# Two ResNet bottlenecks on one core: the Gram stages' transposes shared between TensorE and VectorE

## The chip, the cores and the metric

The kernel runs on one core of a Trainium2 chip, in float32 throughout. The metric is the device time of one execution in microseconds. The kernel before takes 2050.02 us, the median of 3 runs (2049.8 to 2051.2). In what follows PE is TensorE, PEld its loading of weights, DVE is VectorE, ACT is ScalarE, POOL is GpSimd and SP is SyncE, which here only issues transfers.

## The reference

Two bottleneck blocks in a row on a batch of 64 images of 14x14 pixels and 1024 channels (12,544 pixels in all). Each block is, with the batch's own statistics in every normalization:

```python
out = relu(bn(conv1x1(x,   w1) + b1))      # 1024 -> 256
out = relu(bn(conv3x3(out, w2) + b2))      # 256 -> 256
out = bn(conv1x1(out, w3) + b3)            # 256 -> 1024
x   = relu(x + softplus(residual_scale)[0] * out)

# bn: (x - mean) * rsqrt(var + 1e-5) * gamma + beta, mean and var over batch and pixels
```

The third normalization needs mean and variance of the 1024 outputs of the last convolution. The kernel doesn't compute these outputs for that purpose. With z the 256 inputs of that convolution, the variance of an output with weights w is w' G w less the squared mean, where G is the Gram matrix of z over all pixels (256x256) divided by their number. A constant c = max(be2, 0) is taken off z first, which changes no variance and keeps the numbers small.

## The kernel before

All 12,544 pixels of z lie in SBUF as `y_all`, channels on the partitions (two halves of 128). The Gram matrix needs the pixels on the partitions, since TensorE sums over partitions. So each block has a **Gram stage**: 49 times, two blocks of 128 pixels are transposed (four 128x128 transposes on TensorE into a PSUM bank), VectorE copies the bank to an SBUF tile `zt` and takes off c (a row `crow`, loaded by a transfer), and TensorE multiplies `zt` with itself.

```python
def gram(psum, pool, aff, crow, beside):
    g0, g1 = psum.tile(M + 1, "cp"), psum.tile(P + 1, "ap")
    zts = [... for i in range(NZT)]                      # NZT = 4; the last column of each is 1
    def products(k, zt):
        for c in range(CH):                              # CH = 2 blocks of 128 pixels
            nc.tensor.matmul(g0, zt[:, c, 0:P], zt[:, c, :], ...)       # L867: 257 columns
            nc.tensor.matmul(g1, zt[:, c, P:M], zt[:, c, P:], ...)      # L868: 129 columns
    for k in range(NT):                                  # NT = 49
        while normed < NG and normed * GPX < (k + 3) * CH * P:
            ...  norm(s, y_all[:, s, a:b], aff)          # L487, ScalarE: relu(scale * y + shift), 1568 pixels
        tp = psum.tile(CH * M)
        for c in range(CH):
            for s in range(MS):
                nc.tensor.transpose(tp[...], y_all[:, s, px], ident)    # L885
        zt = zts[k % NZT]
        nc.vector.tensor_tensor(zt[:, :, :M], tp..., crow..., ALU.subtract)   # L887
        if before is not None:
            products(*before)
        if k in beside:
            beside[k]()
        before = k, zt
```

`beside` is other work that is put between the pairs: in the first block's Gram stage GpSimd prepares the transformed 3x3 filters of the second block, four pieces (`filters`, lines 160 to 211: some 36 additions and scalings, six results that are sent to HBM as `u`), and at pair 44 VectorE forms sums of w1 and w3 (`combine`, lines 138 to 141) for the fast products that follow. The first block's own filters are prepared by VectorE, half a piece at a time, beside the first convolution. After the Gram stage `conv3_stats` makes mean and variance from G, then the stage follows that does the last convolution of block 0 and the first of block 1 together (`fused`); in block 1 it is the last convolution alone (`final`). In both, GpSimd adds some of the partial sums (lines 425, 430 and 451):

```python
def after7(self):
    u3 = self.saved(...)                                                   # L278, ScalarE, from PSUM
    nc.gpsimd.tensor_add(self.part(1, 1), self.part(1, 1), u3)             # L425
def after3(self):
    self.add(0, 1, self.p)                                                 # L404, VectorE
    nc.gpsimd.tensor_add(v, v, self.u12)                                   # L430
```

The call in the main loop:

```python
crow = pool.tile([P, M], FP, tag="crow", name="crow")
nc.sync.dma_start(out=crow, in_=pars[b][:, NPAR:])
tc.keep_in_program_order(nc.vector.tensor_scalar(crow, crow, 0.0, None, ALU.max))
def piece(s, o):
    spare = [xpool.tile([P, CS * PX], FP, tag="x", name="spare") for i in range(2)]
    for _ in filters(nc.gpsimd, 1, s, o, spare):
        pass
...
beside = {NT - 5: combined}
if b == 0:
    beside.update({1 + 12 * i: partial(piece, i // MS, i % MS) for i in range(MS * MS)})
grams = gram(psum, pool, aff, crow, beside)
made = [conv3(psum, 0, o, w3) for o in range(2)]
...
conv3_stats(psum, pool, grams, w3, ccol, mv3)
```

Where an instruction isn't in `keep_in_program_order`, a scheduler decides when the kernel is built in which order an engine's instructions stand; each engine then runs its list in that order.

Of the kernel before, what the change touches and what calls it, by code (L numbers as in the profile page):

```python
# [38 lines left out]
P = 128  # L40
# [12 lines left out]
NT = NPX // (CH * P)  # L53
NZT = 4
# [26 lines left out]

NROW = M
# [3 lines left out]
def bottlenecks(ctx: ExitStack, tc: tile.TileContext, x, w1s, w2s, w3s, pars, out):  # L86
# [40 lines left out]
    def load_w1(pool, b):  # L127

        w = pool.tile([P, MS, 2, CS // 2, P], FP, tag="w1", name=f"w1_{b}")
        for h in range(2):  # L130
            for o in range(MS):
                nc.scalar.dma_start(out=w[:, o, h], in_=w1s[b][:, o, h])
        return w

    def combine(pool, name, a):

        s = [pool.tile(a[0][0].shape, FP, tag=f"{name}s{i}", name=f"{name}s{i}") for i in range(4)]
        tc.keep_in_program_order(nc.vector.tensor_add(s[0], a[1][0], a[1][1]))
        nc.vector.tensor_sub(s[1], s[0], a[0][0])
        tc.keep_in_program_order(nc.vector.tensor_sub(s[2], a[0][0], a[1][0]))  # L140
        nc.vector.tensor_sub(s[3], a[0][1], s[1])
        return a, s

    def combine_w1(pool, w):
        return combine(pool, "w1", [[w[:, o, h] for h in range(2)] for o in range(MS)])

    def combine_w3(pool, w):
        n = CS // 2
        return combine(pool, "w3", [[w[:, s, o * n : (o + 1) * n] for s in range(MS)] for o in range(2)])
# [10 lines left out]
    def filters(eng, b, s, o, spare):  # L160
# [7 lines left out]
        nc.sync.dma_start(out=g, in_=w2s[b][:, s, o])  # L168

        def scaled(to, v, by):  # L170
            eng.tensor_scalar(to, v, by, None, ALU.mult)  # L171

        eng.tensor_tensor(even, g[:, 0], g[:, 2], ALU.add)
        scaled(quad, g[:, 2], 4.0)
        eng.tensor_tensor(quad, quad, g[:, 0], ALU.add)
# [9 lines left out]
        for i, (row, more, op, by) in parts.items():  # L185
# [3 lines left out]
            if more is not None:  # L189
                v = rest[:, :w]  # L190
                eng.tensor_tensor(v, row, more, op)
                row = v
            if i in FOUR:
                r0, r1, r2 = (row[:, k * P : (k + 1) * P] for k in range(3))
                ends = rest[:, w : w + P]
                eng.tensor_tensor(ends, r0, r2, ALU.add)
                eng.tensor_tensor(u[:, SUM], ends, r1, ALU.add)
                eng.tensor_tensor(u[:, DIFF], ends, r1, ALU.subtract)
# [3 lines left out]
            else:  # L202
# [3 lines left out]
                eng.tensor_tensor(  # L206
# [3 lines left out]
            if i == 2:  # L210
                yield
# [643 lines left out]
    def gram(psum, pool, aff, crow, beside):  # L855
# [6 lines left out]
        normed = 0  # L862

        def products(k, zt):
            for c in range(CH):
                first, last = k == 0 and c == 0, k == NT - 1 and c == CH - 1
                nc.tensor.matmul(g0, zt[:, c, 0:P], zt[:, c, :], start=first, stop=last)  # L867
                nc.tensor.matmul(g1, zt[:, c, P:M], zt[:, c, P:], start=first, stop=last)  # L868

        before = None  # L870
        for k in range(NT):
            while normed < NG and normed * GPX < (k + 3) * CH * P:

                px = [normed * GPX, (normed + 1) * GPX]
                if normed == 0:
                    px.insert(1, CH * P)
                for a, b in zip(px, px[1:]):
                    for s in range(MS):
                        norm(s, y_all[:, s, a:b], aff)
                normed += 1  # L880
            tp = psum.tile(CH * M)
            for c in range(CH):
                px = slice((k * CH + c) * P, (k * CH + c + 1) * P)
                for s in range(MS):
                    nc.tensor.transpose(tp[:, (c * MS + s) * P : (c * MS + s + 1) * P], y_all[:, s, px], ident)  # L885
            zt = zts[k % NZT]
            nc.vector.tensor_tensor(  # L887
                zt[:, :, :M], tp.rearrange("p (c m) -> p c m", c=CH),
                crow[:, None, :].to_broadcast([P, CH, M]), ALU.subtract,
            )  # L890
            if before is not None:
                products(*before)
            if k in beside:
                beside[k]()
            before = k, zt
        products(*before)
        return g0, g1

    def conv3_stats(psum, one, grams, w3, ccol, mv):
# [8 lines left out]

        m = one.tile([P, MS, 2], FP, tag="zmean", name="zmean")
        for s, d in ((0, g0[:, M:]), (1, g1[:, P:])):  # L910
            nc.vector.tensor_copy(m[:, s, 1:2], d)
            nc.vector.tensor_add(m[:, s, 0:1], d, ccol[:, s : s + 1])
        quad = psum.tile(3 * CS, "ax").rearrange("p (o k) -> p o k", k=3)
# [14 lines left out]
        for o in range(CS):  # L928
            for s in range(MS):
                matmul(quad[:, o, 0:2], w3[:, s, o, :], m[:, s, :], start=(s == 0), stop=(s == MS - 1))  # L930
        for o in range(CS):
            matmul(quad[:, o, 2:3], q[:, 0, o * P : (o + 1) * P], ones, start=True, stop=True)
        r = small.tile([P, CS, 3], FP, tag="quad", name="quad")
        nc.vector.tensor_copy(r, quad)
        nc.vector.tensor_copy(mv[:, :, 0], r[:, :, 0])
        sq = small.tile([P, CS], FP, tag="sq", name="sq")
        nc.vector.tensor_mul(sq, r[:, :, 1], r[:, :, 1])
        nc.vector.tensor_sub(mv[:, :, 1], r[:, :, 2], sq)
# [158 lines left out]
    with tc.tile_pool(name="first", bufs=1) as one, tc.tile_pool(  # L1097
# [3 lines left out]
        w1 = load_w1(one, 0)  # L1101
# [6 lines left out]
        w1 = combine_w1(one, w1)  # L1108

        for t, xt in enumerate(pair):  # L1110
# [4 lines left out]
        quarters = itertools.product(range(MS), range(MS))  # L1115
        work = itertools.chain.from_iterable(
            itertools.chain(filters(nc.vector, 0, s, o, spare), (None,)) for s, o in quarters
        )

        def items():  # L1120
            for t in range(2, T, 2):
                xs = [load_x(xpool, 0, t + i) for i in range(2)]
                yield Conv1(psum, one, xs, (t, t + 1), w1, par[0], stats1)
                next(work, None)
# [4 lines left out]
    for b in range(2):  # L1129
        pb = par[b]  # L1130
        sp = softplus(pb)
        ccol = keep.tile([P, MS], FP, tag="ccol", name="ccol")
        nc.vector.tensor_scalar(ccol, pb[:, BE2 : BE2 + MS], 0.0, None, ALU.max)
# [5 lines left out]
        with tc.tile_pool(name=f"last_{b}", bufs=1) as one, tc.tile_pool(  # L1139
# [3 lines left out]
            if b == 0:  # L1143
                w1 = load_w1(one, b + 1)
            aff = affine(aggregate(stats2, 0), MS, pb, G2, BE2)
            with ExitStack() as scope:
# [4 lines left out]
                with tc.tile_pool(name=f"gram_{b}", bufs=1) as pool:  # L1151
                    crow = pool.tile([P, M], FP, tag="crow", name="crow")
                    nc.sync.dma_start(out=crow, in_=pars[b][:, NPAR:])
                    tc.keep_in_program_order(nc.vector.tensor_scalar(crow, crow, 0.0, None, ALU.max))

                    def piece(s, o):
                        spare = [xpool.tile([P, CS * PX], FP, tag="x", name="spare") for i in range(2)]
                        for _ in filters(nc.gpsimd, 1, s, o, spare):
                            pass
# [3 lines left out]
                    def combined():  # L1163
                        if b == 0:
                            weights.append(combine_w1(one, w1))
                        weights.append(combine_w3(one, w3))

                    beside = {NT - 5: combined}
                    if b == 0:
                        beside.update({1 + 12 * i: partial(piece, i // MS, i % MS) for i in range(MS * MS)})  # L1170
                    grams = gram(psum, pool, aff, crow, beside)
                    made = [conv3(psum, 0, o, w3) for o in range(2)]
                    mv3 = small.tile([P, CS, nc.vector.BN_AGGR_DIM], FP, tag="mv3", name="mv3")
                    conv3_stats(psum, pool, grams, w3, ccol, mv3)
# [52 lines left out]
```

## Time and profile before

The profiled execution spans 2048.9 us from its first to its last instruction. By stages:

| stage | from, us | length, us | what it does |
|---|---|---|---|
| first convolution, block 0 | 0 | 313 | products of w1, filters of block 0 on VectorE |
| 3x3 convolution, block 0 | 313 | 299 | |
| Gram stage, block 0 | 612 | 96 | transposes and products, filters of block 1 on GpSimd |
| statistics, first tiles | 708 | 47 | |
| fused last and first convolution | 755 | 575 | |
| 3x3 convolution, block 1 | 1330 | 299 | |
| Gram stage, block 1 | 1629 | 92 | |
| statistics, last convolution | 1721 | 327 | |

How to read the views: the page gives the busy time of each engine and the chain of work that ended last, followed back from the last instruction. The groups of instructions give, for a line of the kernel, how often it ran, its total busy time and the mean of one in ns. The table of windows gives busy times within stretches of time. The timeline gives instructions in order of time, those of one line merged, with the idle time before them in brackets and what ended it. Matmuls overlap in the records, so their pace is read from the differences of their starts. A float32 matmul is recorded as two instructions.

### The profile page before, as it was taken

What the parts mean: (1) busy time and instruction counts of PE and PEld (TensorE: products, weight loads), DVE (VectorE), ACT (ScalarE), POOL (GpSimd) and SP (SyncE); (2) the same over time, 40 slices, a digit from 0 to 9 for tenths busy, and PEclk for the clock granted to TensorE, in tenths of its full rate; (3) what the DMA queues carried; (4) which work ended last, traced back from release to release, by engine and by line L of the source; (5) the groups of instructions that cost most, each with busy time, mean ns of one, the idle gap of its engine ahead of it and who ended that gap; (6) DMA issues with size and microseconds to landing.
All of it is one profiled execution on the core that took longest, in us unless ns stands there. A gap on an engine that the chain in (4) does not pass through costs nothing.

```text
span 2048.9 us, 27957 instructions
## 1 busy us (share of the span) xinstructions
PE 1988.1 (97%) x9896; PEld 1679.1 (82%) x9896; DVE 1559.7 (76%) x2892; ACT 906.4 (44%) x1847; POOL 664.2 (32%) x736
## 2 busy tenths in 40 slices
PE   8989999999989979999999999999999899999998
PEld 4555557999989769999999999989999898555554
DVE  6875568999983556777677667699999734799997
ACT  1101114466644035555555555444656530555555
POOL 0100001121219964333333333312121100566665
PEclk9999999999999989999999999999999999999999
DMA  7755525565642254444444444255656420599998
GB/s 274 271 188 185 189 95 165 185 192 179 198 144 89 96 189 158 187 160 189 158 189 160 187 162 185 95 186 184 199 176 203 173 88 1 219 325 337 339 337 298
DMA packets 160890, 385.88 MB, mean 188 GB/s; under 512 B 8560, under 2 KB 129648, under 8 KB 144240
## 3 DMA queue, kind: packets, MB, share of 16 engines
q1 hardware_dynamic: 150720, 315.88, 44.5%
q10 hardware_dynamic: 5904, 51.91, 6.1%
q0 software_dynamic: 4128, 16.32, 2.0%
q8 instruction: 78, 1.28, 0.2%
q14 instruction: 60, 0.49, 0.1%
HBM read 268.21 MB, written 115.87 MB: 187 GB/s over the span
## 4 chain that ended last, share of the span: by engine, by line
PE 73%; DVE 12%; POOL 6%; DMA 4%; issue 3%; ACT 1%; SPq 0%; DVEq 0%; POOLq 0%; ACTq 0%
PE ay L158 14%; PE cy L158 13%; PE ap L158 7%; PE cp L158 6%; PE even L158 5%; PE odd L158 5%; PE m L158 5%; PE l L158 4%; PE ax L158 4%; PE cx L158 4%; POOL spare L171 3%; PE cp L867 2%; DVE x L404 2%; DMA x<-mid 2%; PE ps L158 1%
## 5 line engine op out<-in xcount | busy, mean ns | idle before, releaser
L278 ACT ACTIVATE cu<-cy,scale 128x196 f32<-128x196 f32 (+1 forms) x552 | 257.5, 475 | 297.5 <-PE cy L158 289.9
L543 POOL TENSOR_TENSOR diffs<-r 128x448 f32<-128x448 f32 (+1 forms) x80 | 111.3, 1402 | 616.9 <-DVE r L525 266.9
L278 ACT ACTIVATE x<-x,shift 128x392 f32<-128x392 f32 x368 | 211.9, 614 | 74.9 <-POOL x L430 58.7
L404 DVE SCALAR_TENSOR_TENSOR x<-cp,scale,x 128x196 f32<-128x196 f32 (+1 forms) x368 | 178.0, 484 | 83.1 <-PE cp L158 81.7
L158 PE MATMUL cy<-ct,w3s 128*128 128x196 f32 (+1 forms) x736 | 222.1, 383 | 2.5 <-ACT cu L278 2.5
L425 POOL TENSOR_TENSOR x<-x,cu 128x196 f32<-128x196 f32 (+1 forms) x184 | 167.3, 909 | 172.1 <-ACT cu L278 172.0
L158 PE MATMUL ay<-at,w1s 128*128 128x196 f32 (+1 forms) x752 | 209.7, 382 | 0.6 <-ACT au L278 0.6
L430 POOL TENSOR_TENSOR x<-x,cu 128x392 f32<-128x392 f32 x124 | 125.7, 1014 | 189.5 <-DVE x L404 189.4
L158 PEld LDWEIGHTS ay<-at,w1s 128*128 128x128 f32 x752 | 136.7, 191 | 35.0 <-ACT au L278 1.5
L158 PEld LDWEIGHTS cy<-ct,w3s 128*128 128x128 f32 x736 | 134.0, 191 | 36.9 <-ACT cu L278 4.1
L278 ACT ACTIVATE au<-ay 128x196 f32<-128x196 f32 (+1 forms) x141 | 53.9, 382 | 244.6 <-PE ay L158 223.2
L451 POOL TENSOR_TENSOR x<-x,cu 128x392 f32<-128x392 f32 x120 | 125.0, 1042 | 82.6 <-DVE x L404 77.5
L158 PE MATMUL m<-sums,ua 128*128 128x224 f32 (+1 forms) x752 | 145.5, 336 | 0.0
L158 PE MATMUL cy<-y,w 128*128 128x196 f32 (+1 forms) x416 | 131.2, 403 | 1.9 <-DVE x L948 1.9
L158 PEld LDWEIGHTS m<-sums,ua 128*128 128x128 f32 x752 | 131.4, 189 | 0.2
L404 DVE SCALAR_TENSOR_TENSOR x<-cx,scale,x 128x196 f32<-128x196 f32 (+1 forms) x184 | 89.1, 484 | 51.8 <-PE cx L158 51.6
L158 PE MATMUL cx<-y,w 128*128 128x196 f32 (+1 forms) x404 | 126.2, 398 | 0.0
L867 PE MATMUL cp<-zt 128*128 128x257 f32 x392 | 120.7, 390 | 5.4 <-DVE zt L887 5.4
L158 PE MATMUL even<-v,ub 128*128 128x224 f32 (+1 forms) x640 | 123.8, 334 | 0.8 <-ACT even L637 0.8
L158 PE MATMUL odd<-v,ub 128*128 128x224 f32 (+1 forms) x640 | 123.9, 335 | 0.2
L158 PE MATMUL l<-diffs,ub 128*128 128x224 f32 (+1 forms) x640 | 122.0, 333 | 0.0
L158 PE MATMUL cy<-ct,w 128*128 128x196 f32 (+1 forms) x368 | 111.2, 384 | 6.6 <-ACT cu L278 6.6
(230 smaller groups left out, 4430.4 us busy)
## 6 DMA issues: line engine op xcount, KB each, us to landing
x<-in_x SPq DMA_DIRECT2D x62, 1568.0 KB, 6.6
ub<-u SPq DMA_DIRECT2D x80, 768.0 KB, 4.6
x<-mid SPq DMA_DIRECT2D x32, 1568.0 KB, 10.2
mid<-x ACTq DMA_DIRECT2D x31, 1568.0 KB, 5.1
out<-x SPq DMA_DIRECT2D x124, 392.0 KB, 6.5
ua<-u SPq DMA_DIRECT2D x96, 256.0 KB, 2.9
ub<-u SPq DMA_DIRECT2D x16, 1024.0 KB, 6.1
u<-y POOLq DMA_DIRECT2D x20, 256.0 KB, 7.0
```

Of the source, the lines that this page charges most:

```text
L158: tc.keep_in_program_order(nc.tensor.matmul(*args, **kw))
L171: eng.tensor_scalar(to, v, by, None, ALU.mult)
L278: tc.keep_in_program_order(nc.scalar.activation(*args, **kw))
L404: nc.vector.scalar_tensor_tensor(v, bank, self.scale[:, o : o + 1], v, ALU.mult, ALU.add)
L425: nc.gpsimd.tensor_add(self.part(1, 1), self.part(1, 1), u3)
L430: nc.gpsimd.tensor_add(v, v, self.u12)
L451: nc.gpsimd.tensor_add(v, v, self.u12[:, i * self.n : (i + 1) * self.n])
L543: nc.gpsimd.tensor_sub(diffs, r[:, :, :, :WH], r[:, :, :, WH:])
L867: nc.tensor.matmul(g0, zt[:, c, 0:P], zt[:, c, :], start=first, stop=last)
```

## The change

Three quarters of the pixels are no longer transposed on TensorE. VectorE has a transpose of blocks of 32x32, which leaves each block within its 32 partitions. So 16 transfers within SBUF first move the pixels: from each quarter of the partitions (32 channels) and each of four runs of 384 pixels to a quarter of the partitions of a tile (`home`), so that partition quarter i of the tile holds all 256 channels of run i. A **step** is 4 x 384 = 1536 pixels, enough for six VectorE transposes of 128x512 elements, each of which fills one `zt`. There are six steps in each Gram stage, two homes in turn, 12 pairs ahead of them and one after them still go by TensorE. Ten of the 16 transfers are issued by SP, six by GpSimd.

Since no copy from PSUM is left in which c could be taken off, c is taken off z in place (`less`), and z stays so: ScalarE does it for the large groups of block 0, VectorE for the rest. A constant taken off every z moves each output by a constant, which the normalization removes, so `conv3_stats` gets simpler. `crow` and its transfer go.

The GpSimd work on filters goes too, since GpSimd has transfers to issue: two of the four pieces of block 1 are prepared by VectorE in the first stage (six pieces in place of four, in smaller parts), two by VectorE in the first Gram stage. The weight sums move from pair 44 to the end. Program order is kept for the transposes, products and filters of the Gram stage. There are six `zt` in place of four, and w1 of block 1 is loaded by SP instead of ScalarE.

The core of the diff:

```diff
-NT = NPX // (CH * P)
-NZT = 4
+NZT = 6
+FIRST, LAST = 12, 1
+RUN = 3 * P
+STEP = 4 * RUN
+STEPS = (NPX - (FIRST + LAST) * CH * P) // STEP
 ...
-    def gram(psum, pool, aff, crow, beside):
+    def gram(psum, pool, homes, aff, less, beside):
 ...
+        bounds = [0, CH * P, 3 * CH * P, *range(GPX, NPX + 1, GPX)]
+        for a, e in zip(bounds, bounds[1:]):
+            for s in range(MS):
+                y = y_all[:, s, a:e]
+                norm(s, y, aff)
+                less(s, y)
+
+        def spread(k):
+            x = homes[k % 2][:, : MS * STEP].rearrange("p (s j f) -> p s j f", s=MS, j=4)
+            for i, j in itertools.product(range(4), range(4)):
+                queue = nc.gpsimd if (4 * i + j) % 8 in (2, 5, 7) else nc.sync
+                a = start + k * STEP + i * RUN
+                queue.dma_start(out=x[32 * i : 32 * i + 32, :, j], in_=y_all[32 * j : 32 * j + 32, :, a : a + RUN])
+            return x.rearrange("p s j f -> p (s j) f")
+
+        def by_tensor(a):
+            tp = psum.tile(CH * M)
+            ...                                  # four transposes on TensorE, kept in program order
+            zt = next(zts)
+            nc.vector.tensor_copy(zt[:, :, :M], tp.rearrange("p (c m) -> p c m", c=CH))
+            return zt
+
+        def by_vector(x, i):
+            zt = next(zts)
+            tc.keep_in_program_order(
+                nc.vector.transpose(
+                    zt[:, :, :M].rearrange("p b (n c) -> p b n c", c=32),
+                    x[:, :, i * CH * 32 : (i + 1) * CH * 32].rearrange("p n (b r) -> p b n r", r=32),
+                )
+            )
+            return zt
+
+        def pairs():
+            for i in range(FIRST):
+                yield by_tensor(i * CH * P)
+            for k in range(STEPS):
+                x = ready.pop(0)
+                for i in range(RUN // (CH * 32)):
+                    yield by_vector(x, i)
+                if k + 2 < STEPS:
+                    ready.append(spread(k + 2))
+            for i in range(LAST):
+                yield by_tensor(NPX - (LAST - i) * CH * P)
+
+        ready = [spread(k) for k in range(2)]
 ...
-        quarters = itertools.product(range(MS), range(MS))
+        pieces = [(0, 0, 0), (0, 0, 1), (0, 1, 0), (0, 1, 1), (1, 0, 0), (1, 0, 1)]
+        total, free = (1 + NF) * len(pieces), T // 2 - 1 - CS // MS      # 42 parts over 11 items
 ...
+                    def less(k, y):
+                        if b == 0 and y.shape[-1] == GPX:
+                            nc.scalar.activation(y, y, AF.Identity, bias=minus_c[:, k : k + 1])
+                        else:
+                            nc.vector.tensor_scalar(y, y, minus_c[:, k : k + 1], None, ALU.add)
+                    ws = sums_tile(one, 2 - b)
+                    homes = [x_tile("home") if b else ws.rearrange("p i n -> p (i n)"), x_tile("home")]
 ...
-                    beside = {NT - 5: combined}
+                    beside = {FIRST + STEPS * RUN // (CH * 32): combined}
                     if b == 0:
-                        beside.update({1 + 12 * i: partial(piece, i // MS, i % MS) for i in range(MS * MS)})
+                        second = x_tile("spare")
+                        work = [filters(nc.vector, 1, 1, o, (x_tile("spare"), second), pinned=True) for o in range(MS)]
+                        ...
+                        beside.update({1 + 3 * i: partial(next, work) for i in range(MS * NF)})
```

The cuts leave out the forms of `combine`, `filters` and `conv3_stats` that follow from this.

## The prediction

> **What bounds the kernel now.** I began with the page: busy shares, then the chain that ended last.
>
> ```profile
> PE 1988.1 (97%) x9896; PEld 1679.1 (82%) x9896; DVE 1559.7 (76%) x2892; ACT 906.4 (44%) x1847; POOL 664.2 (32%) x736
> ...
> PE 73%; DVE 12%; POOL 6%; DMA 4%; issue 3%; ACT 1%; SPq 0%; DVEq 0%; POOLq 0%; ACTq 0%
> ```
>
> TensorE works for 97% of the span, so time can come only from PE work removed (31 to 32 us are at stake here, below) or from its 61 us of idleness. The 6% of POOL in the chain is a hint: GpSimd computes little, yet it stands in the way somewhere. To find where, I cut the span into stages (table of windows; columns are the stretch, its length, then busy us of PE, PEld, DVE, ACT, POOL, PE clock, DMA share, GB/s):
>
> ```profile
> 29.60:313.00 283.40, 276.98 (x832) 158.65 (x831) 197.32 (x335) 31.19 (x60) 13.27 (x24) 0.99 0.50 183
> ...
> 612.30:708.30 96.00, 90.22 (x589) 83.05 (x590) 41.33 (x60) 26.04 (x18) 86.64 (x136) 0.95 0.23 86
> 708.30:755.00 46.70, 36.38 (x142) 25.78 (x141) 24.94 (x56) 10.65 (x23) 39.02 (x58) 0.85 0.53 188
> 755.00:1330.00 575.00, 574.72 (x3466) 574.31 (x3464) 403.36 (x895) 312.28 (x733) 217.97 (x244) 1.00 0.43 168
> ...
> 1629.30:1721.50 92.20, 90.22 (x589) 83.06 (x590) 36.56 (x56) 26.04 (x18) 0.00 (x0) 0.95 0.23 95
> ```
>
> The two Gram stages (612 to 708 and 1629 to 1721) are bound by PE, with DVE under half busy and DMA a quarter used: there is room to move work off PE. The 47 us behind the first one lose 10 us of PE. The timeline of PE inside a Gram stage gives the price of one pair of 128-pixel blocks (start, duration, then the group; overlapping durations, so I read the starts):
>
> ```profile
> 643.45 0.60 PE L885 MATMUL cy<-ident,y 128*128 128x128 f32 x4
> 643.89 0.60 PE L867 MATMUL cp<-zt 128*128 128x257 f32 x2
> 644.32 0.39 PE L868 MATMUL ap<-zt 128*128 128x129 f32 x2
> 644.55 0.60 PE L867 MATMUL cp<-zt 128*128 128x257 f32 x2
> 644.98 0.38 PE L868 MATMUL ap<-zt 128*128 128x129 f32 x2
> 645.20 0.60 PE L885 MATMUL ay<-ident,y 128*128 128x128 f32 x4
> ```
>
> One pair takes 645.20 - 643.45 = 1.75 us; its four transposes take 643.89 - 643.45 = 0.44 us, its products 1.31 us. 49 pairs are 85.8 us; the first stage runs from 613.0 to 708.3, 95.3 us, so 9.5 us are losses: 1.63 and 1.83 us of waiting for DVE at 700 and 704 (DVE had put the eight weight sums of L138 to L141 in front of the zt that PE needed), the rest the slow clock and the waits at the start. The second stage, 1630.0 to 1721.45, loses 5.6 us.
>
> Behind the first Gram stage the chain and PE's timeline show:
>
> ```profile
> 742.77 1.83 POOL spare L171 x3
> ...
> 746.06 0.61 POOL x L425
> ...
> 749.16 1.02 PE L158 MATMUL cy<-ct,w 128*128 128x196 f32 x2 [6.62 <-ACT cu L278]
> ```
>
> GpSimd works through four pieces of block 1's 3x3 filters until 745 and only then does the first addition of the residual (L425). PE waits 6.62 us for what hangs on that, and then runs at half clock until 754.9 (the same matmul of 196 columns steps 0.65 us there, 0.33 after), 2.9 us more.
>
> [...] The PSUM read of the same 512 elements, which it replaces, took 0.69 us (L887). [...] whole-width transfers here reach 337 to 339 GB/s in the last stage. [...]
>
> **The change part by part.**
>
> *Transposes.* Of 49 pairs, 12 + 1 stay on PE, 36 go to DVE. PE saves 36 x 0.44 = 15.8 us per stage, 31.6 in both, if it stays fed.
>
> *What feeds it.* A step is six pairs: 1536 pixels x 256 channels x 4 B = 1.57 MB in 16 transfers. PE uses a step in 6 x 1.31 = 7.9 us, so the transfers must bring 200 GB/s. [...] Latency is covered: six zt buffers let DVE be a step ahead, so a home is free when PE begins on it and its next content is due two steps (15.8 us) later. [...]
>
> *DVE.* [...] 36 x 0.65 = 23 us. With 13 copies (8), two filter pieces (10 us each: for four in the first stage the rows are L171 17.2, L191 8.8, L196 to L198 17.2, L173, L175 and L206 6.1 us, 49 in all, of which some 0.07 us of each of 144 instructions overlap with the next) and a few us of subtractions: 55 of 75 us in the first Gram stage. In the second, 16 subtractions of 1568 elements at about 0.9 us (0.36 us for 384 in L171, scaled) in place of the filters: 47 of 75. Not the bound.
>
> *ACT.* Norm took 26.04 us for 25,088 columns, 1.63 us for 1568. In the first stage ACT also subtracts c for seven groups: 14 more of 1.63 us, 49 us in all. Group 2, which step 0 needs, is done 17 us after ACT's start; plus 8 us of transfer, 25. PE gets through its 12 own pairs in 12 x 1.75 + 6 of start = 27. Just in time. FIRST = 12 looks chosen for this.
>
> *No crow.* The first zt waited for the DMA of crow (landing at 632.3, 1.0 us after the transposes were done, similar in the other stage); a subtraction of 0.3 us takes its place: -0.7 us each, -1.5.
>
> *Weight sums at the end.* They stand behind the last zt now, beside the 2.6 us of conv3 that PE does anyway: -3.5 us.
>
> *GpSimd freed.* No filters there any more: -6.6 of waiting, -2.9 of slow clock. I count -8, since the first units of that stage also wait for ACT (1.35 us at 736.7) and will find something else.
>
> *Filters on DVE in the first stage.* Six pieces in place of four, spread over 11 items of 18.4 us: 42 parts x 1.67 us / 11 = 6.4 us an item, beside 10.3 us of its own: 16.7 of 18.4. PE lost 4.8 us there to DVE waiting for a filter's outgoing transfer, and some 3 us of clock. There were three such changes of piece, now five. +2.
>
> Sum: -31.6 - 1.5 - 3.5 - 8 + 2 = -42.6; +3 for the DMA edge, as an expectation: about -40, **2010 us**.
>
> **Rivals.** (a) *The DMA becomes the bound of the Gram stages.* [...] At 120 GB/s a step takes 13 us, each stage grows by 6 x 5 = 30 us: 2070. (b) *DVE or its fixed order becomes the bound.* If a 32x32 transpose of f32 took 1.3 us, 36 would be 47 us, and the first stage 79 of 75: a few us slower there, 2020. (c) *The saving is there but the first stage gives it back*: DVE full to 91%, in program order, stalls at each of five changes of piece; 5 x 3 us would make 2020 to 2025. (d) *GpSimd was not what held the start of the fused stage*, and x's load or ACT takes its place: 8 us less gain, 2018. The chain speaks against it, being GpSimd without a gap for 45 us.
>
> **Range and chances.** 2% is 2009.0 us, right at my estimate. If all goes as in the sum without the DMA term, 2007; the terms that can fail (a mild, c, d) are each worth 8 to 15 us and have about one chance in four each, and they only add. 1999 would need more from clock and first stage than I count. So 1999 to 2030; faster by over 2%: 0.44, within: 0.51, slower: 0.05, which is rival (a) in earnest.
>
> **What would show it.** Right: Gram stages of about 75 us each with PE products stepping 1.31 us per pair without waits on zt; L885 at 104 instead of 392 transposes; DVE transposes near 0.65 us; step transfers of under 8 us; no PE wait over 2 us between 720 and 760. Wrong: PE waiting for DVE zt which waits for the DMA into home or ws (rival a); DVE busy without gaps in the Gram stage (b); PE waits on DVE y or at in the first 313 us above 8 us (c); a 5 us hole at the start of the fused stage (d).

## The result, and the profile after

| | before | after |
|---|---|---|
| time, median of 4 runs (lowest to highest) | 2049.91 us (2048.19 to 2051.2) | 2023.49 us (2021.36 to 2026.12) |
| ratio, with its 95% interval | 1 | 0.9872 [0.9855, 0.9889] |
| profiled span | 2048.9 us | 2022.6 us |

The changed kernel is 26.4 us faster, 1.3%. The prediction's range held it; its point, 2010, asked for 40 us, so 13.6 us of the expected gain are missing. The page of the changed kernel, busy times and the chain that ended last:

```profile
PE 1955.8 (97%) x9608; PEld 1647.0 (81%) x9608; DVE 1603.2 (79%) x3070; ACT 927.8 (46%) x1865; POOL 599.5 (30%) x648
...
PE 51%; DVE 8%; DMA 4%; SPq 1%; issue 1%; ACT 1%; POOL 0%; DVEq 0%; ACTq 0%; POOLq 0%
```

TensorE lost 32.3 us of busy time (1988.1 less 1955.8) with the 288 transposes that are gone (9896 less 9608 instructions); the time fell by less. GpSimd is out of the chain. Now the same five stages as in the prediction, by windows (stretch, its length, then busy us of PE, PEld, DVE, ACT, POOL, PE clock, DMA share, GB/s):

```profile
29.60:318.50 288.90, 277.19 (x830) 158.12 (x829) 214.65 (x416) 30.62 (x60) 19.76 (x36) 0.99 0.54 195
617.80:703.80 86.00, 75.82 (x445) 67.86 (x446) 56.68 (x141) 47.05 (x34) 25.96 (x48) 0.95 0.77 237
703.80:740.30 36.50, 33.81 (x142) 23.50 (x141) 22.96 (x56) 10.71 (x23) 4.21 (x5) 0.91 0.20 82
740.30:1315.30 575.00, 574.71 (x3466) 574.32 (x3464) 403.27 (x895) 311.74 (x733) 218.17 (x244) 1.00 0.43 166
1617.90:1694.60 76.70, 73.59 (x445) 66.48 (x446) 49.08 (x72) 26.16 (x20) 23.25 (x36) 0.96 0.68 206
```

The two Gram stages do the same products, yet the first has 86.0 us for 75.8 us of TensorE work, the second 76.7 for 73.6. VectorE is at 66% in the first, and still something there waits. Where nothing waits, a pair steps exactly as predicted. TensorE's timeline (start, duration, group), the first products of two pairs in a row:

```profile
661.58 0.60 PE L167 MATMUL cp<-zt 128*128 128x257 f32 x2
...
662.89 0.60 PE L167 MATMUL cp<-zt 128*128 128x257 f32 x2
```

From 661.58 to 662.89 is 1.31 us, a pair without its transposes. The ledger, read from starts of TensorE's instructions at the stage borders (first 3x3 matmul, first transpose of each Gram stage, first conv3 matmul behind it, first matmul of the fused stage's steady part, end):

| stretch | before | after | difference |
|---|---|---|---|
| start to the first 3x3 matmul | 317.1 | 322.6 | +5.5 |
| 3x3 convolution of block 0 | 295.9 | 295.9 | 0 |
| first Gram stage | 95.3 | 85.3 | -10.0 |
| from there to the fused stage's steady part | 48.8 | 38.6 | -10.2 |
| fused stage and 3x3 convolution of block 1 | 873.0 | 876.3 | +3.3 |
| second Gram stage | 91.45 | 76.0 | -15.5 |
| the rest | 327.5 | 328.0 | +0.5 |
| sum (entries are rounded) | 2048.9 | 2022.6 | -26.3 |

Two entries miss the prediction by much: the first Gram stage (75 expected) and the first stretch (+2 expected). The +3.3 does not come again: the twelve other profiles below, in which that stretch's code is the same, have 872.9 to 876.0, eleven of them under 875.

**The first Gram stage.** The timeline of all engines there, cut to VectorE's lines, with TensorE's answer as the last:

```profile
638.69 0.69 DVE L910 COPY zt<-cy 128x512 f32<-128x512 f32 x1 [1.06 <-PE cy L904]
640.44 0.69 DVE L910 COPY zt<-ay 128x512 f32<-128x512 f32 x1 [1.06 <-PE ay L904]
...
644.97 0.70 DVE L916 STREAM_TRANSPOSE zt<-ws 128x512 f32<-128x512 f32 x1
...
646.67 1.41 DVE L189 TENSOR_TENSOR spare<-spare 128x384 f32<-128x384 f32 x4
...
650.65 1.89 DVE L916 STREAM_TRANSPOSE zt<-ws 128x512 f32<-128x512 f32 x3
...
651.41 1.22 PE L167 MATMUL cp<-zt 128*128 128x257 f32 x2 [3.58 <-DVE zt L916]
```

Through the last six of the twelve pairs that TensorE transposes, VectorE idles 1.06 us in each. Behind them stands a heap of filter parts (L186, L189), from 645.6 to 650.65 between the second and the third 32x32 transpose, and TensorE waits 3.58 us for it. Behind the wait it also has less clock, 0.83 granted from 650 to 660 us where the 10 us before have 1.00, by estimate from these two 1.7 us more. The filter parts and the transposes are held in program order, the copies L910 are not: the scheduler put parts behind copies in front of which they were written.

**The start of the fused stage.** The timeline of all engines: GpSimd's first addition there, and TensorE where it had waited 6.62 us:

```profile
732.95 1.10 POOL L442 TENSOR_TENSOR x<-x,cu 128x196 f32<-128x196 f32 x1 [2.06 <-ACT cu L295]
...
735.64 0.49 PE L167 MATMUL ay<-x,w 128*128 128x196 f32 x2
...
736.55 0.60 PE L167 MATMUL cy<-ct,w 128*128 128x196 f32 x2 [0.42 <-ACT cu L295]
```

GpSimd's addition waits for its data now, not the data for it; the hole is 0.42 us. A second loss is gone that the prediction had not seen. In the kernel before, TensorE also waited here:

```profile
730.79 1.55 PE L158 MATMUL cy<-y,w 128*128 128x392 f32 x4 [1.89 <-DVE x L948]
```

VectorE's chain from the sums of the statistics to the first use of their result took 7.3 us there (722.2 to 729.5), with GpSimd at its filters beside it; in the changed kernel it takes 3.2 us (718.5 to 721.7), and 3.2 in the run all by TensorE below, where GpSimd has no filters either. One scaling of 128x8 elements in it (L1177, now L1231) took 1.02 us before and takes 0.23 and 0.22.

**The first stage.** From the table of waits up to 322 us (engine and group waited for, us in total, times, longest):

```profile
DVE y L189 <- DMA u<-y: 14.1, 3, 6.9
...
PE ap L167 <- DVE y L346: 10.5, 5, 4.9
```

In the kernel before, the same two rows had 6.8 us (once) and 5.2 us (twice).

### The profile page after: what moved, and what is told of

The parts are those of the page before. It is cut to its first block, busy times and chain, and to the rows that moved or that the text cites. A ratio compares the mean times of both kernels' runs of the same rounds, so it can differ in the third digit from the quotient of the medians.

```text
span 2022.6 us, 27698 instructions
## 1 busy us (share of the span) xinstructions
PE 1955.8 (97%) x9608; PEld 1647.0 (81%) x9608; DVE 1603.2 (79%) x3070; ACT 927.8 (46%) x1865; POOL 599.5 (30%) x648
## 4 chain that ended last, share of the span: by engine, by line
PE 51%; DVE 8%; DMA 4%; SPq 1%; issue 1%; ACT 1%; POOL 0%; DVEq 0%; ACTq 0%; POOLq 0%
PE cy L167 13%; PE ay L167 9%; PE cp L167 8%; PE ap L167 5%; PE cx L167 4%; DMA x<-mid 3%; PE even L167 3%; PE odd L167 3%; PE ax L167 3%; PE m L167 2%; PE l L167 2%; DVE x L421 1%; DMA out<-x 1%; SPq L896 1%; DVE x L479 1%
## 5 line engine op out<-in xcount | busy, mean ns | idle before, releaser
L421 DVE SCALAR_TENSOR_TENSOR x<-cp,scale,x 128x196 f32<-128x196 f32 (+1 forms) x368 | 177.9, 483 | 82.4 <-PE cp L167 81.3
L167 PE MATMUL cy<-ct,ws 128*128 128x196 f32 (+1 forms) x736 | 221.8, 383 | 2.5 <-ACT cu L295 2.5
L167 PE MATMUL ay<-at,ws 128*128 128x196 f32 (+1 forms) x752 | 209.3, 381 | 1.0 <-ACT au L295 1.0
L167 PEld LDWEIGHTS ay<-at,ws 128*128 128x128 f32 x752 | 136.6, 190 | 35.4 <-ACT au L295 1.9
L167 PEld LDWEIGHTS cy<-ct,ws 128*128 128x128 f32 x736 | 133.6, 190 | 36.9 <-ACT cu L295 3.8
L167 PE MATMUL ap<-x,ws 128*128 128x196 f32 (+1 forms) x376 | 107.5, 390 | 10.2 <-DVE y L346 10.2
```

Of the source, the lines that this page charges most:

```text
L167: tc.keep_in_program_order(nc.tensor.matmul(*args, **kw))
L421: nc.vector.scalar_tensor_tensor(v, bank, self.scale[:, o : o + 1], v, ALU.mult, ALU.add)
```

## The experiments

All times are medians against the kernel before on the same chip; stage lengths come from the one profile of each run, read at the same borders as in the ledger. A stage begins with its first transpose, so a wait in front of that is not in its length.

| run | time (ratio, 95% interval) | first 3x3 matmul at | first Gram | second Gram |
|---|---|---|---|---|
| after | 2023.49 (0.9872 [0.9855, 0.9889]) | 322.6 | 85.3 | 76.0 |
| copies in order | 2060.58 (1.0046 [1.0031, 1.0061]) | 325.5 | 99.4 | 98.6 |
| no filters in Gram | 2013.83 (one run) | 319.9 | 80.7 | 75.2 |
| all by TensorE | 2038.78 (0.9944 [0.9929, 0.9959]) | 322.3 | 89.7 | 90.6 |
| own scratch | 2028.75 (0.9904 [0.9887, 0.9921]) | 326.8 | 85.5 | 76.1 |
| -c apart | 2024.42 (0.9867 [0.9852, 0.9882]) | 323.1 | 85.2 | 77.3 |
| apart and copies | 2021.8 (0.9853 [0.9838, 0.9867]) | 325.2 | 81.3 | 78.0 |
| four pieces | 2018.34 (0.9836 [0.982, 0.9853]) | 315.75 | 86.2 | 75.9 |
| scratch in turns | 2016.59 (0.9826 [0.9811, 0.9841]) | 315.2 | 85.8 | 77.2 |
| turns, apart, copies | 2012.63 (0.9814 [0.98, 0.9828]) | 313.7 | 81.9 | 77.3 |
| c on GpSimd | 2019.2 (0.9839 [0.9822, 0.9856]) | 316.9 | 90.2 | 76.75 |
| one queue | 2036.57 (one run) | 314.1 | 92.6 | 88.7 |
| even queues | 2018.78 (0.9838 [0.9822, 0.9855]) | 313.7 | 90.1 | 75.6 |

### What the transposes are worth: all by TensorE

```diff
-FIRST, LAST = 12, 1
+FIRST, LAST = 48, 1
```

No steps of transfers are left then, only the rest of the change.

> All 49 pairs are transposed by TensorE, with no step of transfers and no 32x32 transposes; the rest of the change (c subtracted from z, filters away from GpSimd, weight sums at the end) stays. Theory: the 36 transposes of a pair are worth 36 x 0.44 = 15.8 us a stage, so the second Gram stage goes from 76.0 to about 91.8; the first, where 9.9 us were lost to VectorE's heap, goes from 85.3 to about 93, and the time to about 2047, so that all else in the change together is worth only about 3 us (GpSimd freed -10, first stage +5.5, the loss at the second block +3). Rival (the waits and not the transposes made the gain): the second stage stays under 85 and the time under 2035.

The second Gram stage took 90.6 us, so the 36 transposes moved to VectorE are worth 14.6 us there (15.8 expected). The first took 89.7, so there they are worth 4.4 us only: this is where the gain went. I had expected 93 for that stage and 2047 in all; it came to 2038.78. Of the 8 us, 3.3 are this stage's: with a copy for every pair the filter parts fell between the copies by themselves and no wait for zt was left in it. Another 2.7 are the stretch in block 1, where the +3.3 is gone, and 1.2 the second stage (91.8 expected). So the rest of the change, which I had put at 3 us, brings 11.5 (2050.28, the kernel before on that chip, less 2038.78).

### Is it the order on VectorE? Copies in order

```diff
-            nc.vector.tensor_copy(zt[:, :, :M], tp...)
+            tc.keep_in_program_order(nc.vector.tensor_copy(zt[:, :, :M], tp...))
```

> The 13 copies of the pairs that TensorE transposes are held in program order on VectorE too, as the filter parts and the 32x32 transposes are already; nothing else differs. Theory (order on VectorE): in the first Gram stage the filter parts of the first twelve pairs were put behind the copies and then stood in one heap of 5 us in front of the third 32x32 transpose; in program order they fit into the 1.06 us that VectorE idles per pair. So that stage falls from 85.3 to 77 to 79 us, TensorE's waits for zt there from 8.7 us to under 2, and the time from 2023.5 to about 2016; the second Gram stage stays at 76. Rival (transfers): the steps are paced by 16 transfers that take about 10 us from first issue to landing, for 7.9 us of products; then the waits only move to the transposes that wait for the transfers, the stage stays at 84 to 86 and the time at 2023.

It came to 2060.58, slower than the kernel before. Waits in that run, of VectorE in the first Gram stage and of TensorE in the second:

```profile
DVE minus_c L1180 <- ACT y L1201: 18.6, 1, 18.6
...
PE cp L167 <- DVE zt L911: 24.4, 1, 24.4
```

The edit removed the heap and made two new waits. In the first stage an instruction of 0.17 us that belongs to the next block (its -c, written into the one buffer that both blocks share) stood in VectorE's queue in mid-stage and could run only when ScalarE had read the old -c for the last time; everything behind it stood for 18.6 us. In the second stage the ordered copies came behind all 16 subtractions of c, and those wait for ScalarE's norm one after the other. So this run tells nothing for or against the order as the cause; it shows what one misplaced instruction of 0.17 us cost in VectorE's queue: 18.6 us for all that stood behind it. The changed kernel has that stray instruction too, with 4.08 us of idle before it, which raised a second theory:

```profile
664.88 0.17 DVE L1178 TENSOR_SCALAR minus_c<-par 128x2 f32<-128x2 f32 x1 [4.08 <-ACT y L1199]
```

### Is it the stray instruction? -c apart, then with the copies

```diff
-        minus_c = keep.tile([P, MS], FP, tag="minus_c", name="minus_c")
+        minus_c = keep.tile([P, MS], FP, tag=f"minus_c_{b}", name="minus_c")
```

> The -c of the two blocks get a buffer each; in the changed kernel they share one, and the 0.16 us instruction that writes the second block's -c was put into VectorE's queue in the middle of the first Gram stage, where it must wait until ScalarE has read the first block's -c for the last time (VectorE idle 4.1 us before it at 665 us; 18.6 us in the run with the copies in order). Nothing else differs. Theory (a stray instruction in the queue): the first Gram stage falls by 2 to 4 us, from 85.3 to 81 to 83, the time to about 2020.5; VectorE's wait for ScalarE before that instruction is gone. Rival (transfers pace the stage): VectorE then waits 4 us for the transfers into home and ws in its place, and the stage and the time stay within 1 us of 85.3 and 2023.

The stage stayed at 85.2 us, the time within 1 us. The rival's numbers were right. The wait for ScalarE is gone and the stage as long as it was, so those 4 us of idle were not on the path: VectorE's 32x32 transposes now stand 5.1 us for a home's transfer and 5.1 for TensorE to give a zt back. The next run adds the copies in order, in the first Gram stage alone:

> A buffer for each block's -c, as in the run with that alone, and the copies from PSUM in program order in the first Gram stage only (in the second, that order had put all 16 subtractions ahead of the first copy and cost 24.4 us). Theory (order on VectorE): the filter parts go into the 1.06 us gaps between copies, the heap of 5 us in front of the third transpose goes away and so does the stray instruction; the first Gram stage takes 77 to 80 us, the second stays at 76, the time is about 2016. Rival (transfers): 84 to 86 us and 2023; a stage between 80 and 84 would say that both take part.

81.3 us, between the two theories' numbers, where the text had said that both take part. TensorE's waits for zt in that stage, in the changed kernel (first row) and in this run:

```profile
PE cp L167 <- DVE zt L916: 8.7, 6, 3.6
...
PE cp L167 <- DVE zt L918: 3.8, 5, 1.3
PE cp L167 <- DVE zt L910: 2.1, 2, 1.8
```

8.7 us of waiting for 32x32 transposes became 3.8, and 2.1 of waiting for the first copies are new: the heap was worth 4 us in this profile, and the same 4 us appear again between the two later kernels without and with this edit (85.8 and 81.9). By the timed runs alone it isn't settled: the interval 0.9838 to 0.9867 overlaps that of the changed kernel.

### The bound below: no filters in the first Gram stage

```diff
         def scaled(to, v, by):
-            run(eng.tensor_scalar(to, v, by, None, ALU.mult))
+            if not pinned:
+                eng.tensor_scalar(to, v, by, None, ALU.mult)
```

The same for the other helper; the two pieces' loads are replaced by zeros from GpSimd.

> Leaves out work: the arithmetic and the weight loads of the two filter pieces in the first Gram stage; what is stored for them is zeros, so the second block's 3x3 convolution is not the reference's. VectorE has 20 us less in that stage. If VectorE (by its order or by its load) held the products back, the stage takes 76 to 78 us, as the second does. If the transfers did, it stays at 84 to 86. If this run shows 77 and the one with the copies in order shows 77 too, the order was the cause and not the load; if only this one does, it was the load.

80.7 us, but 5.3 of them are my own doing: the transposes of the twelfth pair start 26.65 us after the stage's first, in the changed kernel 21.33. TensorE waited 2.3, 2.0 and 0.5 us there for the first subtractions (0.8 in the changed kernel), and had less clock, 0.50 and 0.75 granted in the stage's first two 8 us against 0.67 and 1.00. The reason for the waits stands in two rows of that run's timeline:

```profile
615.76 6.65 DVE L1203 TENSOR_SCALAR y<-y,minus_c 128x256 f32<-128x256 f32 x3 [0.67 <-ACT y L506]
616.49 2.85 POOL L179 MEMSET spare<- 128x3136 f32 x1
```

Three subtractions of 256 and 512 elements, at most 0.5 us each in other runs, needed 6.65 us beside GpSimd's four memsets, which ran without a gap from 611.2 to 622.1. Less these 5.3 us the stage is at 75.4, close to the predicted length and to the second stage in this run, 75.2. So the stage's loss hangs on the filters. It need not be their 23 us on VectorE alone: this run also issues eleven of their twelve stores at once (622.3 to 628.4 us), ahead of the first step, where the changed kernel has them between the steps.

The order explains 4 us of 10 net. Behind the start it explains more. From the transposes of the twelfth pair to its end the stage took 64.0 us in the changed kernel, 57.7 with the copies in order, 54.1 here, and 54.6 in the changed kernel's second stage. There the order was worth 6.3 us, of which 2.3 were lost again at the start, where the ordered copies came late. About 3 us are left for the filters' load, their stores, and transfers that start late (below); how these divide is not shown.

### The first stage: is VectorE too full, or does it wait?

```diff
+            if odd:
+                g = own.tile([P, 3 * w], FP, tag="g", name="g")
+            u5 = own.tile([P, 4 * P], FP, tag=f"u5_{odd}", name="u5")
...
+        def ahead():
+            made = [filters(nc.vector, *piece, spare, own=one, odd=i % 2) for i, piece in enumerate(pieces)]
+            for i, piece in enumerate(made):
+                for following in made[:2] if i == 0 else made[i + 1 : i + 2]:
+                    next(following)
+                yield from piece
```

This is the second form, scratch in turns; the first, own scratch, had two homes for the loaded weights and one new buffer u5.

> First stage only: the filters' loaded weights get two buffers of their own, each load issued one piece ahead, and the last of the six parts of a piece gets a buffer of its own, so that the next piece need not wait until it is stored; the arithmetic and its amount on VectorE stay. Theory (changes of piece): three waits of VectorE for an outgoing transfer, 14.1 us in all and up to 6.9 each, made TensorE late; without them the first 3x3 matmul comes at 317 to 318 us in place of 322.6 and the time is about 2018.5. Rival (load): VectorE is simply too full there with six pieces in place of four; then the stage stays at 321 to 323 and the time at 2023.

It missed: 326.8 us, later than in any other run. The waits of VectorE tell why:

```profile
DVE u L190 <- DMA u<-u: 18.0, 4, 6.1
```

The sixth part of a piece depends on nothing but the loaded weights, so with those loaded ahead the scheduler drew it forward, and it stood there until the store of the piece before had left the one buffer. A wait had been moved, not removed. Two buffers in turn, and beside it a run that leaves out the two added pieces:

```diff
-filters(nc.vector, *piece, spare) for piece in pieces
+filters(nc.vector, *piece, spare, empty=piece[0] == 1) for piece in pieces
```

> The run with own scratch did not settle the changes of piece: a wait of 18.0 us in four parts for the store of the one new buffer took the place of those taken away, and the stage grew. Here the sixth part of a piece has two buffers in turn and the loaded weights two homes in turn, so no piece waits for a store of the one before it. Theory (changes of piece): VectorE's waits for outgoing transfers are under 3 us in all and the first 3x3 matmul comes at 317 to 320 us, the time is about 2019. Rival (load): VectorE has six pieces in the first 200 us in any case; the waits go but the matmul still comes at 321 to 325 and the time stays at 2022 to 2025.

> Leaves out work: the arithmetic and the weight loads of the two pieces of filters that the change added to the first stage (zeros are stored for them, so the second block's 3x3 convolution is not the reference's); VectorE has four pieces there again, as before the change. Theory: the two added pieces are what makes the first stage 2 to 8 us longer (first 3x3 matmul at 322.6, 325.5, 319.9 and 322.3 us in four runs of the same code, mean 322.6, against 317.1 before); here it comes at 316 to 318.5 and the time is about 2018. Rival: the stage varies by itself from run to run and the pieces are not the cause; then it comes anywhere from 319 to 326.

Without the two pieces' work the first 3x3 matmul comes at 315.75 us, with all six and buffers in turn at 315.2. That is 2 us earlier than the 317 to 320 expected, though one wait for a store, 5.2 us where under 3 were expected, is still there. Waits of scratch in turns:

```profile
DVE y L191 <- DMA u<-y: 5.2, 1, 5.2
...
PE ap L167 <- DVE y L351: 3.7, 1, 3.7
```

The six runs with the changed kernel's first stage have 319.9 to 325.5 us, mean 323.1; the five with buffers in turn 313.7 to 316.9, mean 314.7. The handling of the change of piece is worth these 8.4 us, more than the 6.0 that the change had added. That the load of the two added pieces costs anything is not shown: six pieces with buffers in turn come no later than four without. Four with buffers in turn were not run. Whether the loads issued a piece ahead, the second buffer, or the parts' new spacing (36 over the items, where the loads had counted too and made 42) does more was not tried apart.

### The two together, and three tries at the transfers

Turns, -c apart and copies in order, in one kernel:

> The two edits that moved something, together: scratch in turns for the filters of the first stage, and in the first Gram stage a buffer for each block's -c with the copies from PSUM in program order. If the two causes are separate, their gains add: first 3x3 matmul at 315 to 318 us, first Gram stage 81 to 82, second 76, the time 2012 to 2014 us, a ratio of about 0.981 to the kernel before. If they are the same time counted twice, 2016 to 2018.

2012.63 us; the gains add, as the profile shows with 313.7 us for the first stage and 81.9 for the Gram stage. Its interval, 0.98 to 0.9828, lies wholly under that of the changed kernel, so this version beats both kernels; that it beats scratch in turns alone (0.9811 to 0.9841) is not shown by the times. On it, three edits of how a step of transfers is fed:

```diff
-queue = nc.gpsimd if (4 * i + j) % 8 in (2, 5, 7) else nc.sync
+queue = nc.sync                                        # one queue
+queue = nc.gpsimd if (i + j) % 2 else nc.sync          # even queues
```

> On top of the run with turns, apart and copies: all 16 transfers of a step are issued by SyncE, none by GpSimd. Each issue takes 0.60 us, 16 are 9.7 us or more, for 7.9 us of products. If the issuing queue paces the steps, each of the later five steps is 2 to 3 us late and the second Gram stage grows from 76 to 84 to 90 us, the first from 81 to 88 to 94. If the bytes do (1.57 MB on 32 partitions at a time), the number of queues changes nothing, or takes longer by less than 3 us a stage.

The stages grew to 92.6 and 88.7 us, as the theory of the issuing queue had it. SyncE's queue in the second stage, of this run and then of the kernel with two queues (start, duration, count of issues):

```profile
1629.04 63.88 SPq L901 DMA_DIRECT2D home<-y  x96
```

```profile
1618.38 48.86 SPq L901 DMA_DIRECT2D home<-y  x60
```

96 issues without a gap are 0.67 us each, 16 of them 10.6 us for 7.9 us of products. The DMA engines are busy for 0.62 of their time meanwhile (1650 to 1680 us, at 149 GB/s), so it is not the bytes. With 10 of 16 the queue is done in 8.1 us a step, waits for free homes included. A row of the table of windows of that kernel, 10 us that hold nothing but these transfers:

```profile
1640.00:1650.00 10.00, 9.08 (x56) 8.18 (x55) 2.12 (x4) 0.00 (x0) 3.24 (x7) 1.00 0.90 241
```

> On top of the run with turns, apart and copies: of the 16 transfers of a step 8 are on each queue, in place of 10 on SyncE's and 6 on GpSimd's. Theory (the issuing queue paces the steps, as with one queue): SyncE's share of a step falls from 6.6 us or more to about 5.3, GpSimd's grows from 3.2 to 4.3, so a step lands 1 to 2 us earlier; the first Gram stage, where the second step came late by 1.3 us and later ones by 0.5, falls from 81.9 to 79 to 81 us, the time by 1 to 2 us to about 2011. Rival (with two queues the bytes on 32 partitions pace the steps, or GpSimd's queue is held up by VectorE's work): 82 to 86 us and 2012 to 2016.

It missed: 79 to 81 us were expected for the first stage, and its profile has 90.1; the time rose to 2018.78. The second stage's 75.6 us is no gain that could be told from chance, since nine profiles with the 10 and 6 transfers have 75.2 to 78.0 there. The five times spread from 2013.22 to 2023.65 us, and the profile is of the longest, so the 90.1 us need not hold for the others. GpSimd's queue also carries the stores of the filters in that stage. The run's timeline near the last step:

```profile
670.16 0.52 SPq L125 DMA_DIRECT2D x<-in_x  x1
...
672.39 9.53 SPq L901 DMA_DIRECT2D home<-y  x8
...
681.32 0.53 POOL L901 DMA_DIRECT2D home<-y  x1 [4.67 <-DMA u<-spare]
...
689.48 0.80 PE L167 MATMUL cp<-zt 128*128 128x257 f32 x1 [4.30 <-DVE zt L923]
```

One issue of the last step stood 4.67 us behind a store, and the order of SyncE's queue changed as well: a load of x, 1.6 MB, now goes ahead of the step, and the DMA engines are busy for 90% or more of every 2 us from 672 to 692. These came together, so which of them costs the 8 us stays open.

```diff
+if b == 0 and next(calls) in (2 * 4 + 1, 2 * 5 + 1):
+    nc.gpsimd.tensor_scalar(y, y, minus_c[:, k : k + 1], None, ALU.add)
```

> On top of the run with turns, apart and copies: two of the fourteen subtractions of c that ScalarE does in the first Gram stage (second half of the channels, groups 2 and 3, which the first two steps of transfers read) are done by GpSimd. Theory (the first steps start late because ScalarE norms and subtracts, 6.2 us a group): step 0 starts about 1.5 us earlier, step 1 about 3 us, the waits of 1.2 us for the second step's transposes go, the stage falls from 81.3 to 79 to 80 us and the time by 1 to 2.5 us. Rival (GpSimd's work and its queue's transfers get in each other's way, or the steps are paced by their own 10 us): no change, or up to 2 us more.

It missed: the stage took 90.2 us in the profile, which is of the longest of four runs (2014.46 to 2022.28). The run's timeline:

```profile
624.97 4.24 POOL L1216 TENSOR_SCALAR y<-y,minus_c 128x1568 f32<-128x1568 f32 x1 [16.54 <-ACT y L509]
625.04 4.44 DVE L191 TENSOR_SCALAR spare<-spare 128x256 f32<-128x256 f32 x2
...
630.69 1.20 PE L167 MATMUL cp<-zt 128*128 128x257 f32 x2 [3.38 <-DVE zt L915]
```

Two scalings of VectorE that take 0.43 us in the changed kernel stood for as long as GpSimd's subtraction ran, 4.44 us beside 4.24, and TensorE behind them for 3.38 us. The run without filters shows the like, 6.65 us beside the memsets. What stretched them is not shown. It is not all of the 8.3 us: near 682 us TensorE waits 3.22 us more, for a 32x32 transpose that itself stood 5.31 us for a home's transfer, and that this hangs together with the first is not shown.

## Why the prediction was right or wrong

- **What binds, and the price of a pair: right.** TensorE at 97% before and after; a pair 1.31 us; 104 transposes left (L904); the 32x32 transpose 0.67 us where it doesn't overlap (0.65 predicted, the author's estimate; the PSUM read that it replaces took 0.69).
- **The transposes' saving: right in the second Gram stage** (76.0 us against 75; 14.6 us by the run all by TensorE against 15.8), **wrong in the first** (85.3 against 75). The step that failed is "55 of 75 us ... Not the bound". The sum itself was good, VectorE was busy for 56.7 us; but a sum over a stage does not say whether work is there when the engine is free. The filter parts missed the idle of the first twelve pairs, and stood in front of transposes that were due every 1.31 us. Rival (b) named "its fixed order" and tied it to a slower transpose; the order alone was enough for 4 us net, and all filters there, with their stores, for 10.
- **The feed: mostly right.** TensorE waits 1.6 us for zt in the second stage. But the edge was put in the wrong place. That the transfers would run just at the 200 GB/s needed was the author's estimate. With two queues the trace shows 241 GB/s in a 10 us stretch that holds nothing but these transfers (1640 to 1650 us, kernel with the two edits); the DMA engines are busy for 0.90 of it, so at 1.00 it would be about 268 (an estimate from these two numbers). What binds first, when one queue issues all, is the issuing, 0.67 us for each of 96; the prediction did not count it. Rival (a) did not come.
- **ScalarE just in time: right.** ScalarE's subtractions of the group that step 0 needs end near 634.1 us, 16.7 us after its start (17 predicted).
- **Weight sums at the end: right.** No wait for a zt is due to them; goff waits 0.2 us. What leaving out crow saves was not measured by itself; in the run all by TensorE the second Gram stage is 0.9 us shorter than before (0.7 predicted). The landing that the prediction gives as 632.3 is at 1632.3 us, in the second stage; in the first it is at 615.2.
- **GpSimd freed: right, and larger:** -10.2 us against -8, the hole 0.42 against 6.62 us. Beside the hole, VectorE's chain of 7.3 us, now 3.2, and the 1.89 us that TensorE waited for it went too. The run all by TensorE has the same 38.6 us with no VectorE transposes at all, so the transposes are not the cause. That it is the filters' leaving GpSimd rests on the chain and on GpSimd's timeline; no run put only them back. Rival (d) fell.
- **The first stage: the term "+2" was mis-sized.** It measured +5.5 in the profile, +6.0 as a mean of six. The prediction counted load, 16.7 of 18.4 us, and five changes of piece at little cost; the changes turned out to be what costs, and no cost of the load is shown. (The sum took the six loads of weights for parts of arithmetic: 36 parts in place of 42 are 5.5 us an item, 15.8 of 18.4.) That is rival (c), at 6 of its 15 us, and it turned out to be avoidable: with scratch in turns the stage is 2.4 us shorter than before the change.
- **The sum.** Expected -40. First Gram stage short by 10 us, first stage by 3.5, the stretch in block 1 by 3.3 in this profile, against 2 more from GpSimd and 3 that the expectation had set aside for the DMA, the author's estimate: about 12 of the 13.6 that are missing. The range held by its width, which left room for one or two of the failing terms that it names.

## What to carry to other kernels

When work is moved to an engine with room, check the gaps and not only the sum: VectorE was busy for 66% of the first Gram stage, and TensorE still waited 3.58 us there for a heap of short parts that stood ahead of what was due. Pinning some of the instructions lets a scheduler pile the others around them. Before blaming load for a stall between pieces of repeated work, give what is stored and loaded at the seam a second buffer; if a wait moves to the new buffer, as 18.0 us did here, give that one two as well. And count a transfer's issues as time on the queue that issues them: 16 took 10.6 us on SyncE's.

## What was not expected of the hardware

- A 32x32 transpose of 128x512 f32 on VectorE takes 0.67 us, the PSUM copy of as many elements 0.69.
- Transfers of 96 KB between two sets of 32 partitions take 0.67 us each to issue on SyncE (96 in a row) and 0.53 on GpSimd, and a few us to land (medians of 3.4 to 4.0 in the changed kernel's first Gram stage); on two queues they ran at 241 GB/s, with the DMA engines busy for 0.90 of those 10 us.
- Two tensor_scalar of VectorE took 4.44 us beside GpSimd's subtraction of 4.24 (0.43 in the changed kernel), three 6.65 us beside GpSimd's memsets of 2.7 to 2.9 us each (at most 0.5 each in other runs). In the kernel before, beside GpSimd's filters, a scaling of 128x8 took 1.02 us; in the changed kernel it takes 0.23.
- The first stage of one and the same code varied by 5.6 us between six profiles (319.9 to 325.5), so a single profile does not carry a difference of 3 us there.
